# Attention scores of three turns in two visits of three looks, in a two-layer network on one Trainium2 core

## The chip, the cores and the metric

The kernel runs on one core of one Trainium2 chip. The metric is the time of one execution on the device in microseconds (us), the median of several runs. The core's engines are called as in the profile: PE (TensorE, the matrix engine; PEld is its weight load), DVE (VectorE), ACT (ScalarE), POOL (GpSimd) and SP (SyncE, whose queue issues most DMAs). PE writes to PSUM, which has eight banks of 128 partitions x 512 float32 values. DVE and ACT read PSUM; POOL doesn't.

## The reference, cut to what matters

The input is x of 16 images x 512 tokens x 128 values. Each of two layers adds two branches to x. Layer 0 has a memory that is trained along the sequence (the scan) beside a block of convolution, full attention and experts, through all of which every token goes. Layer 1 has two causal attentions, the second with queries made from the first one's output, beside a mixture of 32 experts with 8 for each token.

```python
# layer 0, second branch (B, S, D = 16, 512, 128; 16 heads of 8)
scores = jnp.einsum('bhqd,bhkd->bhqk', q, k) / jnp.sqrt(jnp.float32(dh))
attn = jax.nn.softmax(scores, axis=-1)
ctx = jnp.einsum('bhqk,bhkd->bhqd', attn, v)
...
x = layernorm(x + attn_out, ln1_g, ln1_b)
probs = jax.nn.softmax(x @ gate_w + gate_b, axis=-1)
h = jax.nn.relu(jnp.einsum('bsd,edf->bsef', x, w1) + b1)      # 8 experts, f = 512
y = jnp.einsum('bsef,efd->bsed', h, w2) + b2
moe_out = jnp.einsum('bse,bsed->bsd', probs, y)
x = layernorm(x + moe_out, ln2_g, ln2_b)
...
# layer 1, first branch
ctx = _causal_attn(q, k, v)
conv_out = jax.lax.conv_general_dilated(ctx_c, conv_w, ...) + conv_b[None, :, None]
q2 = conv_out.transpose(0, 2, 1).reshape(b, s, NUM_HEADS, HEAD_DIM)
ctx2 = _causal_attn(q2, k, v)
```

## The kernel before

**Turns.** The whole program is written out by stages that are Python generators. `Turns.run` (line 280) steps every live stage once in each turn, in the order of its level: level 0 is `tops` with `largest` (row maxima of scores), level 1 is `back` with `weighted` (exponentials and values), level 2 `summed` (what is left of an attention), level 3 the scan and later the mixture of layer 1, level 4 projections and what stands between attentions, level 6 layer 0's experts (`experts0`, `ffn`). PE executes its instructions in just the order in which they are written; the other engines' orders come from the compiler's scheduler, which follows the written order where it can. `issue_after` puts what an engine does for later levels behind the last maximum (DVE) and the last causal mask (POOL) of the turn.

**Looks.** An attention of one image is done in two halves of eight heads. A half takes 16 looks in layer 0 and 11 in layer 1, where `widths` shortens them to the causal part (512, 384, 256 and 128 columns, with 1, 1, 2 and 4 pairs of heads to a look). There are two kinds of look, and every score is computed twice. The first kind, in `largest` (tile s, out of kx and qx), is two PSUM banks of scores, whose row maxima DVE takes (lines 391 to 399). The second, in `weighted` (tile s, out of qx and kx), is two banks of transposed scores, from which ACT makes the exponentials e (line 471), which POOL masks in layer 1 (line 475). Both kinds are matmuls of 64 rows, in pairs that use the upper and the lower half of the array. A lock ("p1", "p2") lets one `largest` and one `weighted` at a time take looks, and each yields after a look; so a turn has one look of each kind.

**Values.** `tail` multiplies the exponentials of four or eight (head, key block) pieces with the values (`values`, tile pc, 32 columns of the array to each head), once enough wait in `old`: four in layer 0, eight later (`pools["heads"]`). pc has a PSUM bank of its own, which the lock "ctx" hands from one half to the next. e has three buffers, six from the start of layer 1 on.

**PSUM.** The other seven banks are one pool (`work`, tag "bank"). What keeps a bank over a turn's end is counted by `hold` and `drop` in `held[0]`; `room` holds a stage back when `pools["work"]` (3, at the end 2) are held.

**Experts of layer 0.** `ffn` takes images in order, once their attention is done (mark "x1"). An image has 64 units: 32 `first` (two matmuls of 512 columns, tile phe, then ACT's relu to hTe, line 585) and 32 `second` (eight matmuls of 128 columns, tile pye, line 595; pye is held over four of them). How many units a turn gets follows from a credit: each turn adds TURN = 2750 ns and takes off `load_ns`, an estimate of what the turn's other matmuls cost PE, and 1000 for each unit. Units go in pairs; a turn with values gets none, or four and more. A second rule gives a turn units for as long as DVE is taken to be busy with the look (`look_ns`). `middle` of layer 1 needs an image's experts (mark "ffn"), so these set when layer 1 can begin with an image.

**Fill.** Where no experts run, `fill` (line 198) adds a matmul without use to a turn that has little work for the whole array.

The lines of `ffn` that the change touches:

```python
credit[0] = min(credit[0] + TURN - load_ns[0], 4000)
more = int(max(credit[0] + 500, 0) // 1000)
if pools["pairs"]:
    more = more // 2 * 2 if "values" not in locks or more > 3 else 0
if credit[0] > -2000:
    more = max(more, int((look_ns[0] - load_ns[0] - 400) / 1000 + 0.7))
```

Of the kernel before, what the change touches and what calls it, by code (L numbers as in the profile page):

```python
# [17 lines left out]
P = 128  # L18
# [64 lines left out]
def network(ctx: ExitStack, tc: tile.TileContext, a, out):  # L83
# [56 lines left out]
    pools, done, locks, clock, newest, cleared, held, read, cell = {}, {}, set(), [0], [None], [None], [0], [0], []  # L140

    lent = set()

    def mark(*m):
        done[m] = clock[0]
# [31 lines left out]
    def work(name):  # L177
        return pools["ps"].tile([P, 512], F32, tag="bank", bufs=7, name=name)
# [94 lines left out]
    class Turns:  # L273
# [6 lines left out]
        def run(self, until=None):  # L280
            while (self.stages or self.live) and (until is None or not until()):
                self.live += [x[1:] for x in self.stages if x[0] <= self.turn]
                self.stages = [x for x in self.stages if x[0] > self.turn]
                self.live.sort(key=lambda x: x[0])


                newest[0] = cleared[0] = None
                step = lambda x: next(x[1], StopIteration) is not StopIteration
                left = [x for x in self.live if x[0] == 0 and step(x)]
                with ExitStack() as behind:  # L290
                    if newest[0] is not None:
                        behind.enter_context(tc.issue_after(newest[0].ins))
                    left += [x for x in self.live if x[0] == 1 and step(x)]
                    if cleared[0] is not None:
                        behind.enter_context(tc.issue_after(cleared[0].ins))
                    left += [x for x in self.live if x[0] > 1 and step(x)]
                self.live = left
                self.turn += 1
                fill()
                held[0] -= read[0]  # L300
                read[0] = 0
                load_ns[0] = look_ns[0] = 0.0
                locks.discard("values")
                clock[0] = self.turn

# [68 lines left out]
    def largest(slot, causal):  # L374
# [4 lines left out]
        nm = att.tile([P, TB, 2, NH], F32, tag="nm", bufs=2, name="nm")  # L379
        for i, n, per, t in widths(causal):  # L380
            qt = TB - 1 - i

            look_ns[0] = {S: 2050, 3 * P: 1800, 2 * P: 2450, P: 3000}[n] if causal else 1750
            sv = [work("s1")[:, 0 : per * n].rearrange("p (i n) -> p i n", i=per) for r in range(2)]
            for u in range(per):
                for r in range(2):
                    rr = slice(64 * r, 64 * r + 64)
                    mm(sv[r][:, u, :], q[rr, t + u, qt * P : (qt + 1) * P], k[rr, t + u, :n])
            for r in range(2):
                if causal and per == 1:  # L390
# [8 lines left out]
                newest[0] = nc.vector.tensor_reduce(nm[:, qt, r, t : t + per], sv[r], AX.X, ALU.max)  # L399
            yield  # L400
# [22 lines left out]
    def weighted(slot, vp, c, causal, cn, name):  # L423
# [30 lines left out]
                for _ in range(min(len(old) // 4, 2)):  # L454
                    values([old.pop(0) for _ in range(4)])

        for i, (kt, n, per, t) in enumerate(widths(causal)):
            while len(old) >= pools["heads"] and not got and "ctx" in locks:
                yield
            s = [work("s2")[:, 0 : per * n] for r in range(2)]  # L460
            sv = [x.rearrange("p (i n) -> p i n", i=per) for x in s]
            for u in range(per):
                for r in range(2):
                    rr = slice(64 * r, 64 * r + 64)
                    mm(sv[r][:, u, :], k[rr, t + u, kt * P : (kt + 1) * P], q[rr, t + u, S - n :])
# [13 lines left out]
            for u in range(per):  # L479
                for r in range(2):  # L480
                    old.append((kt, n, t + u, r, ev[:, r, u, :]))
                    if pool is pools["mid"]:
                        lent.add(id(old[-1]))
            yield
        locks.remove("p2")
        free_slots.append(slot)
# [44 lines left out]
    def ffn(b):  # L531
# [79 lines left out]
        while at < len(units):  # L611

            at_ffn[0] = clock[0]
            credit[0] = min(credit[0] + TURN - load_ns[0], 4000)
            more = int(max(credit[0] + 500, 0) // 1000)
            if pools["pairs"]:
                more = more // 2 * 2 if "values" not in locks or more > 3 else 0
            if credit[0] > -2000:

                more = max(more, int((look_ns[0] - load_ns[0] - 400) / 1000 + 0.7))  # L620
            for fn, u in units[at : at + more]:

                if held[0] >= pools["work"] - (fn is second and u % 4 == 0):
                    break
# [986 lines left out]
```

## Time and profile before

| | us |
|---|---|
| median of 3 runs (3653.25 to 3662.67) | 3657.85 |
| the profiled execution | 3651.91 |
| its span, from the first to the last instruction | 3650.2 |
| PE busy | 3434.7 |
| DVE busy | 2281.3 |
| ACT busy | 2218.7 |
| POOL busy | 1586.1 |

The profiled execution is 5.9 us under the median. Three stretches differ. To about 1650 us layer 0's attention runs, with the scan and, from about 200 us, with the experts. From 1650 to 3080 us layer 1's attention runs with the rest of the experts. From 3080 us on no unit of the experts is left, and the last images' attention runs with layer 1's mixture and with `fill` (98.8 us of PE's time from 3080 to 3600 us).

In a timeline each line is a run of like instructions of one engine: its start and its length in us, the engine, the line of the kernel, the operation, out<-in, the shape, and in brackets an idle time ahead of it with what ended it. Ends of matmuls are modelled and overlap what follows, so PE is best read from start to start. "s<-kx,qx" is a look for maxima, "s<-qx,kx" a look for exponentials.

### The profile page before, as it was taken

The page shows a single profiled execution, that of the slowest core. Times are in us where ns is not written, and L with a number is a line of the kernel's source. Part 1 is how long each engine was busy: PE and PEld are TensorE (multiplying, and loading weights), DVE is VectorE, ACT ScalarE, POOL GpSimd, SP SyncE. Part 2 cuts the span into 40 slices and gives each one's busy share as a digit, 9 for nine tenths or more (in the row PEclk, how much of TensorE's full clock was granted, in tenths as well). Part 3 has the DMA queues.
Part 4 walks back from the last instruction along what each step waited for, and adds up shares of the span by engine and source line. Part 5 has one row for each costly group of instructions (what it writes and reads, how often), then busy time and mean ns, then how long its engine had stood idle before and what let it go on. Part 6 is the DMA issues. An engine that isn't in the chain of part 4 may idle for free. (4 is left out here: it accounts for less than half of the span.)

```text
span 3650.2 us, 64197 instructions
## 1 busy us (share of the span) xinstructions
PE 3434.7 (94%) x22191; PEld 1917.4 (53%) x22191; DVE 2281.3 (62%) x5907; ACT 2218.7 (61%) x4919; POOL 1586.1 (43%) x2524
## 2 busy tenths in 40 slices
PE   6999999899999999999999999999999999998887
PEld 3445555455555555455555555565555665443443
DVE  5676656566756565565366666666666666877762
ACT  1566756665666787665666666666666666553443
POOL 5433532432441455432444344434443444443674
PEclk7999999999999999999999999999999999998988
DMA  5222222222223233343444444444344433333343
GB/s 173 69 70 75 73 77 74 69 75 84 64 71 92 89 112 96 114 126 97 128 114 124 121 120 121 121 124 126 104 129 121 129 103 112 107 104 94 85 92 87
DMA packets 290083, 370.91 MB, mean 102 GB/s; under 512 B 46016, under 2 KB 141408, under 8 KB 289376
## 3 DMA queue, kind: packets, MB, share of 16 engines
q1 hardware_dynamic: 282592, 359.99, 34.0%
q0 software_dynamic: 7168, 6.82, 1.1%
q8 instruction: 178, 2.92, 0.3%
q14 instruction: 145, 1.19, 0.1%
HBM read 236.85 MB, written 133.25 MB: 101 GB/s over the span
## 5 line engine op out<-in xcount | busy, mean ns | idle before, releaser
L471 ACT ACTIVATE e<-s 128x512 f32<-128x512 f32 (+1 forms) x2432 | 1273.5, 576 | 568.5 <-PE s L196 512.2
L399 DVE TENSOR_REDUCE nm<-s 128x1 f32<-128x512 f32 (+2 forms) x1408 | 907.1, 683 | 505.7 <-PE s L196 504.4
L391 DVE CUSTOM_DVE_ANT_0 s<-s,sb_const 128x512 f32<-128x512 f32 (+1 forms) x1024 | 624.2, 643 | 432.6 <-PE s L196 427.4
L475 POOL TENSOR_SCALAR_AFFINE_SELECT e<-e 128x128 f32<-128x128 f32 (+2 forms) x1408 | 484.6, 371 | 800.0 <-ACT e L471 774.6
L196 PE MATMUL pc<-e,vp 128*32 128x512 f32 (+3 forms) x6144 | 636.9, 506 | 35.7 <-POOL e L475 28.9
L196 PE MATMUL s<-kx,qx 64*128 64x512 f32 (+3 forms) x3072 | 623.9, 430 | 45.6 <-ACT e L471 17.3
L595 PEld LDWEIGHTS pye<-ew,hTe 128*128 128x128 f32 x4096 | 520.1, 193 | 176.5 <-issue 155.0
L196 PEld LDWEIGHTS s<-kx,qx 64*128 64x128 f32 x3072 | 273.7, 188 | 604.9 <-issue 228.8
L595 PE MATMUL pye<-ew,hTe 128*128 128x128 f32 x4096 | 567.1, 282 | 0.6 <-ACT hTe L585 0.5
L196 PE MATMUL s<-qx,kx 64*128 64x512 f32 (+3 forms) x3072 | 534.4, 357 | 27.5 <-DMA qx<-top 9.4
L196 PE MATMUL phe<-x1T,ew 128*128 128x512 f32 x1024 | 539.4, 611 | 4.7 <-DVE nm L399 1.2
L585 ACT ACTIVATE hTe<-phe,sb_cols 128x512 f32<-128x512 f32 x512 | 353.9, 692 | 268.9 <-PE phe L196 265.6
L603 POOL TENSOR_TENSOR ac<-ac,y 128x512 f32<-128x512 f32 x128 | 163.7, 1279 | 427.9 <-ACT y L602 387.3
L196 PEld LDWEIGHTS s<-qx,kx 64*128 64x128 f32 x3072 | 305.4, 189 | 77.6 <-ACT e L471 17.2
L398 DVE TENSOR_TENSOR s<-s,sb_const 128x256 f32<-128x256 f32 (+1 forms) x384 | 181.1, 516 | 222.4 <-PE s L196 172.5
L196 PEld LDWEIGHTS pc<-e,vp 128*32 128x32 f32 x6144 | 154.3, 110 | 270.6 <-issue 171.7
L196 PEld LDWEIGHTS phe<-x1T,ew 128*128 128x128 f32 x1024 | 158.1, 192 | 56.2 <-issue 29.8
L602 ACT ACTIVATE y<-pye,pr 128x128 f32<-128x128 f32 x512 | 147.4, 370 | 30.4 <-PE pye L595 26.2
L391 DVE DVE_READ_ACCUMULATOR2_ANT nm<- 128x1 f32 x1024 | 145.2, 142 | 0.0
L203 PE MATMUL fill<-sb_pd,sb_const 128*128 128x512 f32 (+2 forms) x234 | 117.7, 590 | 1.1 <-ACT e L471 0.6
L209 POOL TENSOR_SCALAR rs_t<-ss 128x4 f32<-128x4 f32 (+1 forms) x56 | 11.5, 206 | 226.0 <-ACT sq L262 224.7
L209 POOL TENSOR_SCALAR rs_t<-ln_mv 128x4 f32<-128x4 f32 x64 | 12.7, 198 | 172.2 <-DVE ln_mv L219 169.6
(294 smaller groups left out, 3890.6 us busy)
## 6 DMA issues: line engine op xcount, KB each, us to landing
ew<-in_ew SPq DMA_DIRECT2D x256, 256.0 KB
kx<-rk SPq DMA_DIRECT2D x192, 256.0 KB
qx<-rq SPq DMA_DIRECT2D x128, 256.0 KB
rq<-hi SPq DMA_DIRECT2D x64, 256.0 KB
rq<-lo SPq DMA_DIRECT2D x64, 256.0 KB
rk<-hi SPq DMA_DIRECT2D x64, 256.0 KB
rk<-lo SPq DMA_DIRECT2D x64, 256.0 KB
qx<-r SPq DMA_DIRECT2D x64, 256.0 KB
```

The source lines that it names most:

```text
L196: nc.tensor.matmul(o, lhsT=lhsT, rhs=rhs, start=start, stop=stop)
L203: nc.tensor.matmul(o[:, 0:n], lhsT=ident, rhs=cell[0][:, 0:n], start=True, stop=True)
L209: nc.gpsimd.tensor_scalar(t, src, scale, eps, ALU.mult, ALU.add)
L391: newest[0] = nc.vector.tensor_tensor_reduce(out=sv[r][:, 0, :], in0=sv[r][:, 0, :], in1=row["caus"][:, S - n :], scale=1.0, scalar=-BIG, ...
L398: nc.vector.tensor_tensor(dg, dg, bc(row["caus"][:, S - P :], 1, per), ALU.add)
L399: newest[0] = nc.vector.tensor_reduce(nm[:, qt, r, t : t + per], sv[r], AX.X, ALU.max)
L471: nc.scalar.activation(e[:, r, 0 : per * n], s[r], AF.Exp, scale=SCALE)
L475: cleared[0] = nc.gpsimd.affine_select(out=ev[:, r, :, 0:P], in_=ev[:, r, :, 0:P], pattern=[[0, per], [1, P]], compare_op=ALU.is_ge, fill= ...
L585: nc.scalar.activation(hs[i], ph, AF.Relu, bias=col("fb", i))
L595: nc.tensor.matmul(pye[0][:, t, :], lhsT=h[:, t * P : (t + 1) * P], rhs=w2[e][:, f, :], start=(f == 0 and t == 0), stop=(f == 3), skip_gro ...
L602: nc.scalar.mul(y[:, t, :], pye[0][:, t, :], pr[:, t, e : e + 1])
L603: nc.gpsimd.tensor_tensor(ac, ac, y, ALU.add)
```

## The change

A turn's looks are now handed out as tokens, and three turns make a cycle. In the first turn (kind "first") the maxima get a look, the exponentials get one, and the same `largest` gets a second one. In the second turn (kind "none") nobody gets a look. In the third (kind "second") the exponentials come first, then the maxima, then the same `weighted` again. So three turns still have three looks of each kind, in two visits of PE to scores. A third look is tried only where `held[0]` is at most 1 (`again`); otherwise the turn has one look of each kind as before (kind "one"), and the step of the cycle is tried again in the next turn.

In `weighted` the values (`tail`) and what follows the scores (`finish`: exponentials, masks) are no longer written right behind the look: they are collected in `shots` and written when all the looks of the turn are, the values first.

For layer 0's experts the credit of a turn follows its kind (0.75, 0.75 and 1.5 times TURN; 1 for "one"), the rule on values holds for turns of the kind "one" alone, and an image's first portion is one unit longer, so that later pairs are a `first` and the `second` of the unit before. The time that DVE takes for the second look of a "first" turn is credited to the "none" turn.

```diff
+    tokens, shots, kind, phase, later = {"s1": 0, "s2": 0}, [], ["one"], [0], [0.0]
+    SHARE = {"one": 1.0, "first": 0.75, "none": 0.75, "second": 1.5}
+
+    def token(name):
+
+        while not tokens[name]:
+            yield
+        tokens[name] -= 1
...
-                left = [x for x in self.live if x[0] == 0 and step(x)]
+                left = []
+
+                def go(level, name, n):
+                    tokens[name], who = n, None
+                    for x in [x for x in self.live if x[0] == level]:
+                        had = tokens[name]
+                        if step(x):
+                            left.append(x)
+                            if tokens[name] < had:
+                                who = x
+                    tokens[name] = 0
+                    return who
+
+                def again(who, name):
+                    if who is None or not pools["third"] or held[0] > 1:
+                        return False
+                    tokens[name] = 1
+                    if not step(who):
+                        left.remove(who)
+                    took, tokens[name] = tokens[name] == 0, 0
+                    return took
+
+                kind[0] = "one"
+                if phase[0] < 2:
+                    who = go(0, "s1", 1 - phase[0])
+                    top = newest[0]
+                    go(1, "s2", 1 - phase[0])
+                    if phase[0] == 1:
+                        kind[0], phase[0] = "none", 2
+                    else:
+                        ns, look_ns[0] = look_ns[0], 0.0
+                        if again(who, "s1"):
+                            kind[0], phase[0] = "first", 1
+                        later[0], look_ns[0] = look_ns[0], ns
+                else:
+                    who = go(1, "s2", 1)
+                    go(0, "s1", 1)
+                    top = newest[0]
+                    if again(who, "s2"):
+                        kind[0], phase[0] = "second", 0
                 with ExitStack() as behind:
-                    if newest[0] is not None:
-                        behind.enter_context(tc.issue_after(newest[0].ins))
-                    left += [x for x in self.live if x[0] == 1 and step(x)]
+                    if top is not None:
+                        behind.enter_context(tc.issue_after(top.ins))
+                    for end in {id(p[0]): p[0] for p in shots}.values():
+                        end(pools["heads"])
+                    for _, finish, args in shots:
+                        finish(*args)
+                    shots.clear()
...
-                load_ns[0] = look_ns[0] = 0.0
+                load_ns[0], look_ns[0], later[0] = 0.0, later[0], 0.0
...
         for i, n, per, t in widths(causal):
             qt = TB - 1 - i
-
+            yield from token("s1")
...
-        for i, (kt, n, per, t) in enumerate(widths(causal)):
-            while len(old) >= pools["heads"] and not got and "ctx" in locks:
-                yield
...
-            tail(pools["heads"])
+        def finish(i, kt, n, per, t, s):
...
+        for i, (kt, n, per, t) in enumerate(widths(causal)):
+            while len(old) + 2 * len(shots) >= pools["heads"] and not got and "ctx" in locks:
+                yield
+            yield from token("s2")
...
+            shots.append((tail, finish, (i, kt, n, per, t, s)))
             yield
...
-            credit[0] = min(credit[0] + TURN - load_ns[0], 4000)
+            credit[0] = min(credit[0] + TURN * SHARE[kind[0]] - load_ns[0], 4000)
...
-                more = more // 2 * 2 if "values" not in locks or more > 3 else 0
+                more = more // 2 * 2 if "values" not in locks or more > 3 or kind[0] != "one" else 0
...
-            for fn, u in units[at : at + more]:
+            for fn, u in units[at : at + more + (at == 0 and more > 0)]:
...
-    pools.update(ps=ps, work=3, weights=[att], mid=None, heads=4, pairs=True)
+    pools.update(ps=ps, work=3, weights=[att], mid=None, heads=4, pairs=True, third=True)
```

More of the change, by code (lines that the diff above doesn't have):

```diff
@@ L455, in tail @@
                     values([old.pop(0) for _ in range(4)])
-        for i, (kt, n, per, t) in enumerate(widths(causal)):
-            while len(old) >= pools["heads"] and not got and "ctx" in locks:
-                yield
[L460 to L465, printed above, removed]
-            tail(pools["heads"])
+        def finish(i, kt, n, per, t, s):
             pool = pools["weights"][i % len(pools["weights"])]
@@ L483, in weighted @@
                         lent.add(id(old[-1]))
+        for i, (kt, n, per, t) in enumerate(widths(causal)):
+            while len(old) + 2 * len(shots) >= pools["heads"] and not got and "ctx" in locks:
+                yield
+            yield from token("s2")
+            s = [work("s2")[:, 0 : per * n] for r in range(2)]
+            sv = [x.rearrange("p (i n) -> p i n", i=per) for x in s]
+            for u in range(per):
+                for r in range(2):
+                    rr = slice(64 * r, 64 * r + 64)
+                    mm(sv[r][:, u, :], k[rr, t + u, kt * P : (kt + 1) * P], q[rr, t + u, S - n :])
+            shots.append((tail, finish, (i, kt, n, per, t, s)))
             yield
```

## The prediction

> **What bounds the kernel now.** I read the busy times first, then the same by stages, then PE's timeline inside the stages.
>
> ```profile
> span 3650.2 us, 64197 instructions
> PE 3434.7 (94%) x22191; PEld 1917.4 (53%) x22191; DVE 2281.3 (62%) x5907; ACT 2218.7 (61%) x4919; POOL 1586.1 (43%) x2524
> ...
> L471 ACT ACTIVATE e<-s 128x512 f32<-128x512 f32 (+1 forms) x2432 | 1273.5, 576 | 568.5 <-PE s L196 512.2
> L399 DVE TENSOR_REDUCE nm<-s 128x1 f32<-128x512 f32 (+2 forms) x1408 | 907.1, 683 | 505.7 <-PE s L196 504.4
> ```
>
> PE is busy 94%, and the two engines that empty the scores idle mostly for PE's scores. By stages (columns: PE, PEld, DVE, ACT and POOL, then the granted clock and DMA):
>
> ```profile
> 60.00:1650.00 1590.00, 1509.65 (x8742) 818.01 (x8743) 997.15 (x1879) 1033.59 (x2434) 635.04 (x625) 0.98 0.29 84
> 1650.00:3080.00 1430.00, 1408.06 (x10182) 841.76 (x10186) 883.01 (x2727) 914.69 (x1932) 604.46 (x1269) 1.00 0.41 119
> 3080.00:3600.00 520.00, 452.26 (x2972) 224.13 (x2966) 364.01 (x1138) 245.49 (x511) 287.31 (x536) 0.91 0.36 92
> ```
>
> PE idles 80 us in the first stretch, 22 in the second, 68 in the last. While experts run, the time is the sum of PE's starts, so I price the change there. An ordinary visit to the scores, in layer 0:
>
> ```profile
> 1504.00 1.02 PE L196 MATMUL phe<-x1T,ew 128*128 128x512 f32 x2
> 1504.87 1.05 PE L595 MATMUL pye<-ew,hTe 128*128 128x128 f32 x8
> 1505.76 1.02 PE L196 MATMUL phe<-x1T,ew 128*128 128x512 f32 x2
> 1506.71 0.49 PE L196 MATMUL s<-kx,qx 64*128 64x512 f32 x2
> 1507.05 0.40 PE L196 MATMUL s<-qx,kx 64*128 64x512 f32 x2
> 1507.37 1.16 PE L595 MATMUL pye<-ew,hTe 128*128 128x128 f32 x8
> 1508.37 1.02 PE L196 MATMUL phe<-x1T,ew 128*128 128x512 f32 x2
> ```
>
> From start to start, phe takes 0.87 with pye behind it but 0.95 with scores behind it; pye takes 0.89 after phe but 1.00 after scores. The two looks take 0.34 and 0.32. The visit costs PE 0.08 + 0.34 + 0.32 + 0.11 = 0.85.
>
> In a few turns of this trace nothing stands between two visits, and four looks follow each other, in layer 0 and in layer 1:
>
> ```profile
> 1615.15 0.50 PE L196 MATMUL s<-kx,qx 64*128 64x512 f32 x2
> 1615.48 0.39 PE L196 MATMUL s<-qx,kx 64*128 64x512 f32 x2
> 1615.71 0.40 PE L196 MATMUL s<-kx,qx 64*128 64x512 f32 x2
> 1616.43 0.62 PE L196 MATMUL s<-qx,kx 64*128 64x512 f32 x2 [0.32 <-DVE nm L399]
> ...
> 2811.08 0.39 PE L196 MATMUL s<-qx,kx 64*128 64x512 f32 x2
> 2811.31 0.39 PE L196 MATMUL s<-kx,qx 64*128 64x256 f32 x4
> ```
>
> A look between two looks takes 0.23 (1615.48 to 1615.71, 2811.08 to 2811.31). So the first look of a visit carries some 0.11 and the last some 0.09 more than a middle one, beside 0.08 and 0.11 in the neighbours. The fourth look shows the other side: its second bank comes only 1.28 after the visit's start, when DVE has reduced the first one.
>
> **What it removes.** A visit of three looks costs 0.85 + 0.23 = 1.08. Three looks cost 1.5 x 0.85 = 1.275 now, so each visit of three saves 0.195. How many there are depends on the banks held. The column sums give 1216 looks of each kind (1536/2 matmuls of 512 columns, 512/2 of 384, 512/4 of 256, 512/8 of 128), 512 of them in layer 0. I went through PE's order in the trace and counted at each visit the tiles whose matmuls stand ahead of it and whose reader comes in that turn or later (pye counts until its fourth unit). Two or more are held at about 35% of the visits up to 1650 us, 15% to 3080, hardly any after. Stepping the cycle through this list (a blocked turn is one ordinary turn) gives 250, 302 and 139 visits of three in the stretches, 693 in all. Saved: 693 x 0.195 = 135 us. Bounds: nothing, if no third look is allowed; 811 x 0.195 = 158 with all. I take the count.
>
> **What it adds: a wait for banks.** Six banks of scores and one held make seven. What next needs a bank (phe, a transpose, a projection) is ready at 0.34 + 0.23 + 0.33 = 0.90 and gets one at 1.28 by the row above: 0.38 late. Everything on PE queues behind it, the next scores too, and so DVE and ACT. No wait arises where values follow the scores (eight pc matmuls take 1.0, 1501.31 to 1502.30, and have their own bank) or no bank is held. By the thresholds of four and eight pieces about 35% of layer 0's visits and 55% of layer 1's have no values. Of the visits with at most one held, one is held in 72%, 70% and 27%. That makes 250 x 0.35 x 0.72 = 63, 302 x 0.55 x 0.70 = 116 and 139 x 0.55 x 0.27 = 21 waits, 200 x 0.38 = 76 us. Bounds: none (at 2811.31 a look starts at once) and one in each of the 693, 263 us. I take the counted ones, the nearest row being the same pool in the same state.
>
> The Trainium skill, page "TensorEngine Tiling (Array Packing)", section "Performance Considerations", speaks against the change: tiling speeds up the matrix engine and not the emptying of PSUM, which can become the bound. Here two reductions of one look take DVE 1.29 us where a middle look takes PE 0.23. If that rule decided in each visit, the gain of 135 would be gone; by the waits counted above, somewhat over half of it is.
>
> **The visit that follows early.** DVE has both looks of a "first" turn reduced 0.53 + 4 x 0.65 = 3.1 us (layer 1: up to 3.4) after the visit's start (1506.71 to 1507.24, then 1.29 for each look). Half a cycle is 3 x 2.8 / 2 = 4.2 us, with 1650 to 3080 us holding 73 visits in 200 us. An early "second" visit finds its last two banks late; I take 15% of 346 visits at 0.38, 20 us. Bounds: 0, and 0.55 (a third look at 1018.75 idled that long for DVE) in all 346, 190 us. The pairs of relu (0.69) and exponentials (1.09 a look) that ACT has to do fit in the same 4.2 us.
>
> **Moved or reordered at no cost.** Exponentials are written after the values, but ACT can start with the first look as before; the three e buffers of layer 0 are full after every second "second" visit, and then one look's exponentials start about 1 us later, hidden by the 4.2 us to the next use. Without that cover it would be 1.09 for each such visit. Masks in layer 1 end one look (1.09) later in "second" turns, and POOL's other work is queued behind them; POOL is 43% busy, and its readers come three turns later. The values' matmuls, the units (1024) and the fill stay as many: 0.75 + 0.75 + 1.5 is three turns' credit, and fill goes to turns without values, still about half. That a pair now starts with phe is in the wait above. The last look of `largest` may now be followed by its end in the same turn, so the DMAs of the maxima (lines 416 and 420, SP's queue) may be issued a turn earlier; their readers wait five turns as before. No DMA is added; SP's order changes by a turn at most.
>
> **The end.** Starts of stages may meet a "none" turn. For the last image four starts (two halves' maxima, then exponentials, in two attentions overlapped) lose about one turn each at times; I take 4 us, between 0 and 4 x 2 turns x 2.1 us = 17.
>
> **Sum.** 135 - 76 - 20 - 4 = 35 us less than the profiled 3651.9: 3617. The median of the runs stands 5.9 above the profiled one: 3623.
>
> **Rivals.**
> A. The forecast, 3623, own range 3570 to 3646. For it: PE's stretches without idle time and the 0.23 of a middle look. Chance 0.47.
> B. The waits hardly arise: stages leave enough other work behind the scores. Only the 135 counts: 3523 to 3570. For it: after 1650 us PE hardly idles now. Against it: six of seven banks in one visit. Chance 0.12.
> C. Emptying PSUM decides, and the gain is given back: 3647 to 3669. For it: DVE and ACT both over 60% in the first stretch, beside the scan. The same result comes if pye, held through more turns, blocks most third looks. Chance 0.14.
> D. Slower: the third look or the unit behind it waits for a bank in most visits. In the first stretch looks that come third idled 0.55 (1018.75) and 1.36 us (846.35). The point is a mean wait of 0.195 a visit; 0.55 in every second visit is 0.275, or 693 x 0.08 = 55 us of loss: 3713; a mean of 0.25 gives 3696. For it: ACT is often behind in the scan's stage. Against it: most such looks came with two or three banks held, which `again` excludes (the 1.36 came with none). Chance 0.27.
>
> **How the numbers follow.** Two runs of this kernel differ by up to 0.26%, so 0.3% (11 us) is about what can be told from no change. Faster by more: A and B, 0.59. Within: C, 0.14. Slower: D, 0.27. The likeliest is A. From 3560 to 3695 about 0.1 is left out at each end (most of B's part below 3560, D's beyond 3695).
>
> **What would show it.** In the changed trace: about 690 visits of six score matmuls, with a start-to-start time near 0.34, 0.23, 0.33; phe right behind some of them 0.4 late with ACT or DVE as releaser; as many matmuls as before; PE's idle time up by some tens of us; experts ended by about 3050 us. Wrong if: visits of three are under 400 (C), PE's idle time in the first stretch grows from 80 to over 130 us (D), or the experts end in a later turn than before, which would move the whole end.

## The result, and the profile after

The changed kernel takes 3852 us (median of 4 runs, 3843 to 3859) against 3656 us for the kernel before on the same chip: ratio 1.053, 95% interval 1.0505 to 1.056. It is 196 us slower, where 35 us less was forecast. The profiled execution spans 3848.4 us. First the page of the changed kernel, the shares of the engines and the rows that answer to those shown ahead of the prediction (name, count, busy us, mean ns, idle us ahead, releaser):

```profile
PE 3522.7 (92%) x22211; PEld 2001.9 (52%) x22211; DVE 2278.9 (59%) x5907; ACT 2185.0 (57%) x4919; POOL 1585.7 (41%) x2524
...
L513 ACT ACTIVATE e<-s 128x512 f32<-128x512 f32 (+1 forms) x2432 | 1245.5, 580 | 519.8 <-PE s L204 416.2
L450 DVE TENSOR_REDUCE nm<-s 128x1 f32<-128x512 f32 (+2 forms) x1408 | 896.1, 682 | 522.5 <-PE s L204 520.7
...
L204 PE MATMUL s<-kx,qx 64*128 64x512 f32 (+3 forms) x3072 | 627.0, 399 | 55.6 <-DVE nm L450 13.9
...
L204 PE MATMUL s<-qx,kx 64*128 64x512 f32 (+3 forms) x3072 | 618.1, 391 | 33.8 <-ACT e L513 13.3
...
L464 PE MATMUL tpm<-sb_const,mp 128*128 128x128 f32 x96 | 31.0, 323 | 77.8 <-DVE mp L457 77.7
```

The same three groups of PE before the change:

```profile
L196 PE MATMUL s<-kx,qx 64*128 64x512 f32 (+3 forms) x3072 | 623.9, 430 | 45.6 <-ACT e L471 17.3 <-DMA kx<-rk 13.4 <-ACT hTe L585 7.0
L196 PE MATMUL s<-qx,kx 64*128 64x512 f32 (+3 forms) x3072 | 534.4, 357 | 27.5 <-DMA qx<-top 9.4 <-ACT e L471 6.3 <-DVE nm L399 6.0
...
L413 PE MATMUL tpm<-sb_const,mp 128*128 128x128 f32 x96 | 28.4, 296 | 19.1 <-DVE mp L406 17.1 <-ACT y L602 1.2 <-ACT e L471 0.3
```

The work is the same (20 matmuls more, all of them fill), and PE is busy 88 us longer with it. DVE and ACT still idle for PE. One row stands out: the transposes of the maxima (`tpm`) idled 19.1 us in all before and now idle 77.8, nearly all of it for DVE.

By the same stages, with the borders moved to the same points of the work (columns as before: PE, PEld, DVE, ACT, POOL, clock, DMA):

```profile
60.00:1690.00 1630.00, 1546.94 (x8694) 852.28 (x8694) 987.56 (x1872) 1016.31 (x2425) 635.84 (x624) 0.97 0.29 82
1690.00:3220.00 1530.00, 1431.92 (x10112) 869.29 (x10111) 873.12 (x2694) 894.54 (x1921) 600.50 (x1252) 0.98 0.39 111
3220.00:3790.00 570.00, 469.12 (x3053) 244.36 (x3053) 377.19 (x1171) 244.32 (x519) 282.85 (x535) 0.87 0.33 85
```

Layer 0's last half ends at 1747 us instead of 1702, the experts at 3217 instead of 3079, layer 1's last half at 3831 instead of 3632. So 45 us are lost in layer 0 and 154 in layer 1.

Now PE's order. Two visits of three, one behind the other, in layer 0:

```profile
1480.60 0.51 PE L204 MATMUL s<-qx,kx 64*128 64x512 f32 x2
1480.94 0.40 PE L204 MATMUL s<-kx,qx 64*128 64x512 f32 x2
1481.18 0.40 PE L204 MATMUL s<-qx,kx 64*128 64x512 f32 x2
1481.51 1.07 PE L204 MATMUL pc<-e,vp 128*32 128x512 f32 x8
1482.50 0.50 PE L204 MATMUL s<-kx,qx 64*128 64x512 f32 x2
1482.84 0.54 PE L204 MATMUL s<-qx,kx 64*128 64x512 f32 x2
1483.07 0.79 PE L204 MATMUL s<-kx,qx 64*128 64x512 f32 x2
1483.79 1.11 PE L204 MATMUL pc<-e,vp 128*32 128x512 f32 x8
```

The first is the visit that was forecast: 0.34, 0.24, 0.33 us from start to start. The second begins 1.9 us later, and its third look takes 0.72 (1483.07 to 1483.79). No idle time is written beside it: the wait falls between the two matmuls of a look and counts as busy. In layer 0 the third look's median is 0.71 us, and over 0.41 in three of four visits. This is another such visit, with ACT and the weight loads beside PE:

```profile
387.12 1.02 PE L204 MATMUL phe<-x1T,ew 128*128 128x512 f32 x2
...
388.07 0.50 PE L204 MATMUL s<-qx,kx 64*128 64x512 f32 x2
...
388.18 0.69 ACT L639 ACTIVATE hTe<-phe,sb_cols 128x512 f32<-128x512 f32 x1 [1.70 <-PE phe L204]
388.41 0.40 PE L204 MATMUL s<-kx,qx 64*128 64x512 f32 x2
...
388.64 0.78 PE L204 MATMUL s<-qx,kx 64*128 64x512 f32 x2
...
388.92 0.18 PEld L204 LDWEIGHTS s<-qx,kx 64*128 64x128 f32 x1 [0.32 <-ACT hTe L639]
...
389.35 0.82 PE L649 MATMUL pye<-ew,hTe 128*128 128x128 f32 x5
```

An expert's first product (`phe`) is the last thing ahead of the visit. ACT reads its bank until 388.87. Only then does the third look's second matmul load its weights (388.92, with ACT's relu as the releaser), and the look takes 0.71 (388.64 to 389.35) in place of 0.33. Nobody "holds" that bank in the kernel's own count: it is in flight within one turn. Over both layers 392 third looks take more than 0.41 us. The last release inside the look came from ACT in 201 of them (its relu in 120) and from DVE in 39; for the other 152 the trace names none.

To see where the time went I added PE's times from one matmul's start to the next, without the idle time ahead of the next, by kind of work. The kernel as written has 312 cycles of three turns, 624 visits of three; in the trace 571 visits have just three looks, 269 have two, 123 one. The scores take 66 us more than before, fill 9 and all other matmuls 13. Idle time grows by 59 us ahead of `tpm` and by 51 ahead of everything else (more ahead of `phe`, 15, layer 1's projections, 13, other transposes, 17, the looks themselves, 16, and `pye`, 7; less ahead of the values, 8, and of others). These five make the 198 between the two spans. Had the 571 visits saved 0.195 each, 111 us would have come off the scores and the matmuls beside them. These take 66 + 13 more instead, so 190 us of lateness stand there as busy time: waits within a look, and in part a slower clock (last section).

### The profile page after: what moved, and what is told of

The parts are those of the page before. It is cut to its first block, busy times and chain, and to the rows that moved or that the text cites. A ratio compares the mean times of both kernels' runs of the same rounds, so it can differ in the third digit from the quotient of the medians.

```text
span 3848.4 us, 64183 instructions
## 1 busy us (share of the span) xinstructions
PE 3522.7 (92%) x22211; PEld 2001.9 (52%) x22211; DVE 2278.9 (59%) x5907; ACT 2185.0 (57%) x4919; POOL 1585.7 (41%) x2524
## 5 line engine op out<-in xcount | busy, mean ns | idle before, releaser
L513 ACT ACTIVATE e<-s 128x512 f32<-128x512 f32 (+1 forms) x2432 | 1245.5, 580 | 519.8 <-PE s L204 416.2
L450 DVE TENSOR_REDUCE nm<-s 128x1 f32<-128x512 f32 (+2 forms) x1408 | 896.1, 682 | 522.5 <-PE s L204 520.7
L442 DVE CUSTOM_DVE_ANT_0 s<-s,sb_const 128x512 f32<-128x512 f32 (+1 forms) x1024 | 615.9, 651 | 534.4 <-PE s L204 518.5
L204 PE MATMUL s<-qx,kx 64*128 64x512 f32 (+3 forms) x3072 | 618.1, 391 | 33.8 <-ACT e L513 13.3
L204 PE MATMUL phe<-x1T,ew 128*128 128x512 f32 x1024 | 550.4, 622 | 19.3 <-DVE nm L450 6.4
L204 PEld LDWEIGHTS s<-kx,qx 64*128 64x128 f32 x3072 | 319.6, 192 | 350.9 <-issue 109.0
L204 PEld LDWEIGHTS s<-qx,kx 64*128 64x128 f32 x3072 | 315.7, 190 | 309.6 <-issue 114.4
L211 PE MATMUL fill<-sb_pd,sb_const 128*128 128x512 f32 (+2 forms) x258 | 127.1, 584 | 0.8 <-DVE nm L442 0.2
L464 PE MATMUL tpm<-sb_const,mp 128*128 128x128 f32 x96 | 31.0, 323 | 77.8 <-DVE mp L457 77.7
```

The costliest lines, as they stand in the source:

```text
L204: nc.tensor.matmul(o, lhsT=lhsT, rhs=rhs, start=start, stop=stop)
L211: nc.tensor.matmul(o[:, 0:n], lhsT=ident, rhs=cell[0][:, 0:n], start=True, stop=True)
L442: newest[0] = nc.vector.tensor_tensor_reduce(out=sv[r][:, 0, :], in0=sv[r][:, 0, :], in1=row["caus"][:, S - n :], scale=1.0, scalar=-BIG, ...
L464: nc.tensor.transpose(tp[:, 0:P], padded, ident)
L513: nc.scalar.activation(e[:, r, 0 : per * n], s[r], AF.Exp, scale=SCALE)
```

## The experiments

Each edit is shown against the changed kernel; `held[0]` counts the banks held over turns. In e2 and e4 one of the sixteen images, in e3 four, have their first expert's output weighted with gate probabilities that are not yet normalised; the work is the same in number and size.

**e1: no third looks.**

```diff
-    pools.update(..., pairs=True, third=True)
+    pools.update(..., pairs=True, third=False)
```

> No third look anywhere; shots, shares and the longer first portion of experts stay. Three theories for the 196 us lost. Banks: the third look of a visit waits on PE for its second bank (start to start, scores take 952 us in the changed kernel where 885 - 122 = 763 was expected from 624 visits x 0.195, so some 190 us of waits). Maxima: PE idles 78 us instead of 19 ahead of the transposes of the maxima (tpm), because a cycle brings them nearer to the reductions. Order: values and exponentials written after all looks, and the experts' new shares, cost by themselves. Banks and maxima both expect the loss gone: 3640 to 3680. Order expects over 3750.

3660 us against 3658 for the kernel before, ratio 1.0002 (0.9991 to 1.0013). All that the change costs comes with the third looks and the cycle of uneven turns that they start. Writing the exponentials behind the values and the early first unit cost nothing. The shares of the experts are not tested by this: without a third look every turn is of the kind "one", whose share is 1. No run changes them while third looks are on.

**e2, e3, e4: one suspect each.**

```diff
-                    if who is None or not pools["third"] or held[0] > 1:
+                    if who is None or not pools["third"] or held[0] > 0:
```

> A third look only with no bank held (before: at most one). Banks: one bank is spare in each visit of three, so a third look's wait (mean 0.43 us over a free one) falls under 0.1; visits of three fall from 624 to some 250 to 350, and 3852 falls to 3690 to 3760. Maxima: idle time ahead of tpm falls only as far as cycles do, to some 40 us, so 3800 to 3820. Order: no change, over 3830.

3737 us, ratio 1.022 (1.020 to 1.023), a time within 3690 to 3760, but not for the reason given there. The 225 visits of three that are left still wait 0.40 us each beyond the clean 0.90, where under 0.1 was expected, against 0.12 for a visit of two. So it isn't the held bank alone that is missing.

```diff
-            for fn, u in units[at : at + more + (at == 0 and more > 0)]:
+            to = at + more + (at == 0 and more > 0)
+            to += more > 0 and to % 2 == 0
+            for fn, u in units[at:to]:
```

> A portion of experts always ends with a second unit (a portion that would end with phe takes one unit more), so that phe with its relu on ACT never stands right ahead of a visit. Banks held by the phe ahead: visits of three after phe (71 of 1.44 us in layer 0 against 1.10 after pye) lose 0.3 us each in layer 0 and a part of it later, 30 to 60 us in all: 3790 to 3820. Banks in general (the looks' own, held and in use together, whatever stands ahead): within 20 us of 3852. Maxima, order: no change.

3838 us, ratio 1.050 (1.047 to 1.053), 14 us less, as the theory of banks in general had it. The waits for ACT's relu in third looks are gone: it is the last release in 7 late third looks in place of 120. But 364 third looks are still late, after 392, and what comes behind the visit now waits: PE idles 89 us right behind visits of three in place of 44, and `phe` idles 35.0 us in all in place of 19.3.

```diff
         )
-        yield
+        yield from idle(2)
         yield from room()
```

(behind `mp`, at the end of `largest`)

> The transpose of the maxima comes one turn later than in the changed kernel (two turns after the last DVE work on them is written). Maxima: idle time ahead of tpm falls from 78 to under 20 us, and the time by 50 to 60: 3790 to 3805. Banks, order: within 15 us of 3852, as PE would wait elsewhere for the same DVE.

3829 us, ratio 1.047 (1.045 to 1.049), between the ranges of the theories. This is what the edit removes, in the changed kernel's timeline:

```profile
2832.63 1.27 DVE L450 TENSOR_REDUCE nm<-s 128x4 f32<-128x512 f32 x2
...
2833.73 0.50 PE L204 MATMUL s<-qx,kx 64*128 64x512 f32 x2
...
2834.09 0.12 DVE L456 TENSOR_SCALAR mp<-nm 128x32 fp32r<-128x32 f32 x1
2834.20 0.42 DVE L556 TENSOR_TENSOR cn<-tpc,rec 128x256 f32<-128x256 f32 x1
2834.55 0.96 DVE L457 SCALAR_TENSOR_TENSOR mp<-nm,mp 128x32 fp32r<-128x32 f32 x1
2835.65 0.30 PE L464 MATMUL tpm<-sb_const,mp 128*128 128x128 f32 x1 [1.42 <-DVE mp L457]
```

DVE is still at the maxima of the last look and then makes `mp`. `tpm` stands next on PE, one turn later as written, and PE idles 1.42 us. With the edit, two rows of e4's groups of PE's instructions:

```profile
L464 PE MATMUL tpm<-sb_const,mp 128*128 128x128 f32 x96 | 28.7, 299 | 3.9 <-DVE mp L457 3.6
L204 PE MATMUL pjq<-xT,sb_pd 128*128 128x512 f32 x32 | 25.6, 893 | 48.9 <-DMA xT<-xt 48.9
```

74 us of idle time are gone and only 23 us of the time. Layer 1's first projection (`pjq`) now idles 48.9 us for the transfer of its input; it comes three turns behind that transfer's issue. That these turns have become shorter for want of the wait at `tpm` is likely, but wasn't measured.

**e5, e6: one bank less.** The pool has six banks in place of seven, with third looks (e5) and without (e6).

```diff
-        return pools["ps"].tile([P, 512], F32, tag="bank", bufs=7, name=name)
+        return pools["ps"].tile([P, 512], F32, tag="bank", bufs=6, name=name)
```

> The changed kernel with six rotating PSUM banks instead of seven; nothing else differs. Theory 1 (banks set the price of the third look: in a visit of three with seven banks the third look and what follows the visit wait together 0.45 us, because the third look's second bank and the next projection's bank are still being read): with one bank less every third look has to wait for the visit's own first look, whose banks come free some 1.28 us after the visit's start, and the projection behind it waits as well. The 571 visits of three lose another 0.4 to 0.7 us each, so 4050 to 4250 us, and the gap to the next kernel grows from 194 us to 280 us or more. Theory 2 (the loss is the order of the work, in-order queues and distances counted in turns, not the number of banks): the kernel loses about what the next one loses, the gap stays at 150 to 240 us.

> Six rotating banks in the changed kernel with third looks switched off (that form with seven banks measured 3660 us). Theory 1: a visit of two takes four banks, the other two serve the projection and one more tile, so a part of the visits begins to wait; 3690 to 3830 us. Theory 2: if banks are not what binds at all, 3655 to 3690 us in this one, and the other one 3850 to 3930.

4116 us, ratio 1.126 (1.124 to 1.128), and 3819 us, 1.046 (1.044 to 1.048). The gap grows from 192 to 296 us. The groups of looks in e5 (both kinds), then in e6 (one kind):

```profile
L204 PE MATMUL s<-kx,qx 64*128 64x512 f32 (+3 forms) x3072 | 704.7, 408 | 115.5 <-DVE nm L442 27.2 <-DVE nm L450 24.0 <-ACT e L513 20.1
L204 PE MATMUL s<-qx,kx 64*128 64x512 f32 (+3 forms) x3072 | 702.1, 402 | 91.8 <-ACT e L513 37.0 <-DVE nm L450 10.8 <-ACT y L656 10.2
```

```profile
L204 PE MATMUL s<-kx,qx 64*128 64x512 f32 (+3 forms) x3072 | 637.3, 432 | 34.6 <-ACT e L513 15.3 <-DMA kx<-rk 8.9 <-DVE nm L450 3.2
```

With six banks the idle time ahead of the looks more than doubles (207 us for both kinds in e5, 89 in the changed kernel); without third looks that of the first kind, shown for e6, is 35. A visit of three waits 0.86 us (0.45 with seven), a visit of two 0.25 (0.13 with seven). Over 571 and 1144 visits that is 234 and 137 us, most of the measured losses of 264 and 159. Both times and the gap lie where theory 1 put them. So one bank less nearly doubles the wait of a visit of three, and a visit of two already pays a little. What one bank more would give back wasn't tried: the eighth bank is that of the values.

**e7, e8: half of VectorE's maxima.** The maxima of layer 0 over 256 columns of 512, with and without third looks.

```diff
-                newest[0] = nc.vector.tensor_reduce(nm[:, qt, r, t : t + per], sv[r], AX.X, ALU.max)
+                newest[0] = nc.vector.tensor_reduce(
+                    nm[:, qt, r, t : t + per], sv[r] if causal else sv[r][:, :, 0 : n // 2], AX.X, ALU.max
+                )
```

> The changed kernel, with the maxima of the scores without a causal mask (layer 0) taken over 256 of the 512 columns: the other half of each maximum is left out, everything else runs as before, so VectorE's 1024 reductions of 683 ns take about 350 ns. It measures what VectorE's pace has to do with the third look's wait. Theory A (the bank that the third look lacks is the expert's or projection's, held until ScalarE has read it, only now and then one that VectorE reads): layer 0 keeps its loss, the third look's median in layer 0 stays over 0.5 us, and against the next kernel the gap falls from 194 us by 10 to 50 us only, most of it from the idle time ahead of the transposes of the maxima (34 of the 96 lie in layer 0). Theory B (VectorE, one look after another, is late in giving the first look's banks back): the third look falls to 0.33 to 0.45 us in layer 0 and the gap falls by 60 us or more.

> The same maxima over 256 of 512 columns in layer 0 (half of each left out) with third looks switched off, as the base for the run above. Both theories: VectorE is not what ends a visit of two in most places, so 3600 to 3660 us; visits of two in layer 0 lose part of their 0.13 us of wait, 5 to 50 us in all.

3823 us, ratio 1.047 (1.045 to 1.049), and 3631 us, 0.994 (0.993 to 0.996). Two rows of e7's page:

```profile
L450 DVE TENSOR_REDUCE nm<-s 128x1 f32<-128x256 f32 (+2 forms) x1408 | 628.1, 490 | 698.8 <-PE s L204 697.4
...
L466 PE MATMUL tpm<-sb_const,mp 128*128 128x128 f32 x96 | 31.1, 324 | 76.8 <-DVE mp L459 74.4
```

VectorE has 268 us less to do, and both forms win the same 29 us: the gap stays at 192. The third look's median in layer 0 stays at 0.69 (0.71 before), so theory B falls: in layer 0, where the edit acts, VectorE's pace in reducing isn't what makes the third look late. Theory A had the median right, but it also expected a gap smaller by 10 to 50 us, and the gap didn't shrink at all; `tpm` didn't gain, since most of them lie in layer 1. ScalarE's pace, which A names, was not varied.

**e9, e10, e11: clear the places of the waits.** e10 joins the edits of e3 and e4, lets layer 1's projections wait five turns instead of three, and keeps the first expert's weighting behind the gate, as all runs from here on do. e9 also asks that the values follow; e11 also that no bank is held.

```diff
-                    if who is None or not pools["third"] or held[0] > 1:
+                    if who is None or not pools["third"] or held[0] > 1 or not (shots and follow[0]()):
...
         nc.sync.dma_start(xT, xt[1, b])
-        yield from idle(3)
+        yield from idle(5)
...
+            follow[0] = lambda: bool(got or "ctx" not in locks) and len(old) >= pools["heads"]
             while len(old) + 2 * len(shots) >= pools["heads"] and not got and "ctx" in locks:
```

> The changed kernel, but a third look is done only when the product with the values follows the visit in the same turn (it needs no new bank), every portion of experts ends with a second product (so no projection awaits its relu when a visit starts), the end of the maxima comes one turn later, and layer 1's projections wait five turns instead of three for their input. As written 122 triples of turns are left, 244 visits of three instead of 624. Theory (a visit of three costs what the banks around it cost; where they are free it saves 0.195 us): 244 x 0.195 = 48 us saved, and waits of 0.1 to 0.25 us a visit instead of 0.45, 24 to 61 us, so 3630 to 3680 us. Rival (the three-turn rhythm itself costs, through queues and distances, in proportion to its turns): 3655 + 194 x 244/624 = 3730 us, so 3715 to 3745.

> The same as the run above without its condition that the values follow: portions of experts end with a second product, the end of the maxima comes one turn later, layer 1's projections wait five turns; 302 triples, 604 visits of three. If each of these mended a cost of its own, the gains add up: 14 us and 23 us as measured alone, and up to 30 us ahead of the projections, so 3785 to 3800 us. If seven banks are what is short, a wait taken away in one place comes back in another: 3800 to 3835 us, with the visits of three still waiting 0.35 us or more each.

> As the first run of this group, and also only while no bank at all is held over turns: 59 triples, 118 visits of three. Theory: 118 x 0.195 = 23 us saved, waits of 0.1 us or less a visit in the places with most room, 12 us, so 3630 to 3660 us, about the time before the change. Rival (rhythm): 3655 + 194 x 118/624 = 3692 us, so 3680 to 3705.

e9 3785 us (ratio 1.036, 1.034 to 1.038), e10 3760 (1.030, 1.028 to 1.032), e11 3733 (1.022, 1.020 to 1.024). All three miss their ranges. e10 does better than either theory allowed: the three moves are worth 92 us together, where 14 and 23 as measured alone and at most 30 for the third make 67. Part of it is the clock (last section). The rows show that the moves free each other:

```profile
L204 PE MATMUL phe<-x1T,ew 128*128 128x512 f32 x1024 | 556.3, 628 | 29.6 <-ACT e L513 10.5 <-ACT y L657 7.6 <-DVE nm L442 5.4
...
L464 PE MATMUL tpm<-sb_const,mp 128*128 128x128 f32 x96 | 29.3, 305 | 4.2 <-DVE mp L457 4.0
...
L204 PE MATMUL pjq<-xT,sb_pd 128*128 128x512 f32 x32 | 17.8, 639 | 2.4 <-DMA xT<-xt 2.2 <-ACT e L513 0.2
```

Both idle times, of `tpm` and of `pjq`, are gone now, where e4 had exchanged one for the other. The visits of three still wait 0.43 us each (564 of them, 243 us, for a saving of 110), as the banks' theory expected. e9 and e11 are worse than both theories the other way: with 122 and 59 triples of turns left as written, a triple costs 1.1 and 1.4 us (the loss against the kernel before, by the triples), against 196/312 = 0.63 in the changed kernel and 0.36 in e10.

**e12 to e15: the moves alone, the conditions alone.** e12 is e10 without third looks; e13 the condition on the values and e14 that on both, without the moves; e15 only e3's edit without third looks.

```diff
 e12, e15:
-    pools.update(..., pairs=True, third=True)
+    pools.update(..., pairs=True, third=False)
 e13, e14 (e14 with held[0] > 0):
-                    if who is None or not pools["third"] or held[0] > 1:
+                    if who is None or not pools["third"] or held[0] > 1 or not (shots and follow[0]()):
```

> The three moves of the last group (portions end with a second product, the end of the maxima one turn later, layer 1's projections two turns later) with third looks switched off: what the moves cost by themselves. Theory (a distance lengthened for one wait makes another thing late: with the end of the maxima later, the rows that carry the maxima reach the score tiles later, and the second kind of look waits for that transfer): 3690 to 3740 us, idle time ahead of these looks 45 us or more (27.5 before). Rival (a few triples of turns cost much more than their looks): 3645 to 3670 us, as without the moves.

> The changed kernel with the one condition that a third look is done only when the product with the values follows in the same turn; no other move (the first expert's output is scaled only once the gate is normalised). 120 triples, 240 visits of three. Theory: 240 x 0.195 = 47 us saved against 240 x 0.36 us waited (what these visits measured with the moves) = 86, and a part of the idle time ahead of the transposes of the maxima, up to 59 x 240/624 = 23 us: 3680 to 3725 us. Rival (triples cost, however few): 3740 to 3790 us.

> The same, and only while no bank is held over turns: 49 triples, 98 visits of three. Theory: 98 x (0.28 - 0.195) = 8 us lost, and up to 9 us ahead of the transposes: 3655 to 3680 us. Rival: 3690 to 3735 us.

> Only the first of the three moves (portions of experts end with a second product), third looks switched off: 3645 to 3675 us by both, the base for reading the run with all moves; over 3690 us would mean that this move and not the transfers costs the time.

e12 3660 us (ratio 1.0001, 0.998 to 1.002), e15 3662 (1.002, 1.0003 to 1.003): the moves cost nothing by themselves, and my theory for e12 falls. e13 3798 (1.038, 1.035 to 1.042), e14 3730 (1.019, 1.016 to 1.023): the rival's side in both, e13 even 8 us beyond its range. Few triples (120 and 49) cost more each, 1.2 and 1.5 us, than many.

**e16, e17, e18: the order between triples.** While the cycle waits for its second visit of three, the turns between do their looks in turned order, the exponentials' first. e16, e17 and e18 are e9, e11 and e13 with the usual order there (e17 with `held[0] > 0`).

```diff
-                if phase[0] < 2:
-                    who = go(0, "s1", 1 - phase[0])
+                if phase[0] < 2 or held[0] > 1 or not follow[0]():
+                    who = go(0, "s1", phase[0] != 1)
                     top = newest[0]
-                    go(1, "s2", 1 - phase[0])
+                    go(1, "s2", phase[0] != 1)
...
-                        if again(who, "s1"):
+                        if phase[0] == 0 and again(who, "s1"):
```

> The kernel with the three moves and third looks only with the values behind (122 triples, measured 3785 us, while the moves without third looks measured 3660), with one more edit: while a triple waits for its second visit of three, the looks of the turns between are done in the usual order, the maxima's first. In the run before, 525 visits of two had the order turned round and took 0.918 us instead of 0.787 in the kernel without third looks. Theory (the turned order puts VectorE's work late in each such turn): 525 x 0.13 = 68 us come back, and part of the idle time behind, so 3690 to 3725 us. Rival (the triples themselves cost it): 3770 to 3795 us.

> The same edit on the run with 59 triples (only while no bank is held; measured 3733 us; 538 visits of two in turned order at 0.869 us). Theory: 538 x 0.08 = 44 us come back and part of the idle time behind, 3660 to 3695 us. Rival: 3720 to 3745 us.

> The same edit on the run with the condition alone, without the moves (120 triples, measured 3798 us; 483 visits of two in turned order at 0.909 us). Theory: 483 x 0.12 = 58 us come back and part of the idle time ahead of transposes and projections, 3695 to 3745 us. Rival: 3780 to 3810 us.

3764, 3721 and 3780 us (ratios 1.030, 1.017 and 1.033; intervals 1.028 to 1.032, 1.015 to 1.019, 1.031 to 1.035). The turned order accounts for 12 to 21 us (19 to 22 by the ratios, as the kernel before was 6 us slower beside these runs than beside e9 and e11), not for the 44 to 68 that I had worked out: e17 and e18 lie at the edge of the rival's ranges, e16 six us under it. The rest stays. In e17 the 93 visits of three wait 0.25 us, so that saving and wait about cancel, and yet 61 us are lost against e12. Rows of e12 and of e17:

```profile
L204 PE MATMUL s<-kx,qx 64*128 64x512 f32 (+3 forms) x3072 | 628.8, 431 | 32.7 <-DMA kx<-rk 10.0 <-ACT e L513 7.7 <-DVE nm L450 7.1
```

```profile
L205 PE MATMUL s<-kx,qx 64*128 64x512 f32 (+3 forms) x3072 | 626.7, 425 | 62.2 <-ACT e L514 17.7 <-DVE nm L451 13.1 <-DMA kx<-rk 10.2
```

The two profiled spans differ by 58 us. 47 of them are idle time on PE, 30 ahead of the looks for maxima (32.7 to 62.2 us), where the rows name ACT and DVE for 16; 11 are busy time, which a slower clock could account for (last section). Why triples that stand alone cost this stays open. In e16 their first visit begins 2.55 us behind the ordinary one ahead of it (median), but in the kernel before two ordinary visits are only 2.6 us apart too, so that alone doesn't explain it. That the experts' uneven shares cost it wasn't tried either. No version with third looks came near the kernel before.

## Why the prediction was wrong

- **What bounds the kernel** was read rightly: PE's starts. Every loss above is a longer distance between starts, or idle time on PE.
- **What a visit saves** was right in size where nothing is in the way: 0.34, 0.24 and 0.33, with the middle look at 0.23. There were 571 visits of three in place of 693 (its three counts add up to 691), so 111 us in place of 135. An ordinary visit was priced at a clean 0.85; on average one waited 0.13 us more before the change.
- **"What it adds: a wait for banks" is the step that failed first.** I counted a wait only where something was held over turns and no values followed, 200 x 0.38 = 76 us. The banks of the same turn are short too: a `phe` that ACT has not yet read, `pye` during its scaling, the two looks themselves. The visits of three wait 0.45 us on average, with values behind them too (0.46 in layer 0), 571 x 0.45 = 254 us together with what follows. The visits of two waited 0.13 us each before, 1150 x 0.13 = 150 us, and the 269 that are left still wait 43. So waits grew by 147 us, more than the 111 saved, where the sum had 76 + 20. e2 shows that the waits remain where no bank is held over turns, e5 and e6 that a bank less raises them to 0.86, e7 and e8 that in layer 0 DVE's pace doesn't set them. In the row that the 1.28 was read from, the bank that comes at 1616.43 is the fourth look's first, not its second; the 0.38 doesn't change by that.
- **"Moved or reordered at no cost" is the second.** I had seen that the end of `largest` may come in the same turn and looked at its DMAs; not at PE, where `tpm` is queued in order and DVE still has the turn's two looks to reduce. PE idles 59 us more ahead of `tpm`, and 110 us more in all, layer 1's projections and the rest included. e10, with longer distances, has a profiled span 99 us shorter, 49 of it idle time, and e12 shows that these distances are free without third looks.
- **"The visit that follows early"** assumed visits 4.2 us apart. The medians are 4.9 us from a "first" to the next "second" and 3.3 from there to the next "first"; behind an ordinary visit it is 2.7. Visits of three less than 2.5 us behind another wait 0.67 us on average, those 2.5 to 4 us behind 0.32, and those further behind 0.42. So a short distance adds to the wait, but a long one doesn't end it. The 20 us were too little; how much wasn't taken apart from the banks.
- **The end** was priced at 4 us. From the experts' end to the last half it takes 614 us now and took 553, 61 more, with a slower clock in it.
- **A slower clock** is in no term of the sum. The prediction shows the granted clock by stages (0.91 in the last) and puts its change at nothing; an estimate from the traces gives up to 49 us (last section).
- Of the rivals D had the mechanism, a third look or what follows waiting for a bank in most visits, and the sign, with a mean wait of 0.195 to 0.275 us. The mean is 0.45, beside 0.13 in visits of two, and the idle time outside visits was in no rival. Its chance of 0.27 was too small. C, that emptying decides, agrees with the waits for readers of banks; it would have given the gain back and no more.
- The test that I named for D, PE's idle time in the first stretch over 130 us, did not fire: 83 us (1630 less 1547) after 80. The waits stand inside the looks as busy time, and only the distances from start to start show them. The tests on the experts' end (3050 us; it was 3217) and on the third look's time (0.33; 0.71 in layer 0) did.

## What to carry to other kernels

Before work is bunched, count all buffers in use at that point, with those that their reader hasn't finished within the same turn and those that the next step needs; where the count reaches the pool's size, take the whole step at the price of the wait, and run the kernel once with one buffer less to see what a buffer is worth. An order that is written in turns keeps its distances in turns: when turns become uneven, list every step that waits "so many turns" for another engine or a transfer and work out how many microseconds are left. Read waits from the distances between starts, since a wait within a group can stand in the records as busy time. Where the granted clock of two versions differs, price that before the rest is put down to waits.

## What was not expected of the hardware

The granted clock fell from 0.969 to 0.957 over the span, and in the last stretch, where no experts are left, from 0.91 to 0.87. In these traces its record has two values only, 1.0 and 0.5. At 1.0 the matmuls of a `pye` start 0.112 us apart, at 0.5 0.213 us (medians of both kernels). At 0.5 lie 229 us of the span before and 332 us after.

This allows an estimate, from PE's time between starts without idle time: 179 us of it lie at 0.5 before and 277 after. If all of that ran at half speed, the slower clock is worth (277 - 179) / 2 = 49 us of the 198. It is an upper value, since waits that count as busy are in it. In e10 these 277 us are 197 again, so up to 40 of the 99 us between the two spans can be the clock. e12 has 189 and e17 222, up to 17 of the 58 us between their spans. The other runs with few triples (e9, e11, e13, e14, e16, e18) have 244 to 272, up to 33 to 47 us each against the kernel before. A loss that is read as waits alone can be too large by these amounts.

What lowers the clock is not shown by these runs. The amount of idle time on PE alone doesn't order them: e3 idles 326 us and e9 240, with 327 and 338 us at 0.5. Nor was a run made in which the clock stayed the same.
